# Layer 1's first pass in three parts around a run-time branch, with two chunks kept from attention and three tiles loaded early

## The chip, the cores and the metric

The kernel runs on one core of one Trainium2 chip. The metric is the device time of one execution in microseconds (us), as the median of the runs shown; less is better. The profile comes from one further execution of the same program, and every time inside it counts from the start of its span.

## What is computed

The input `x` is an image of 256 x 256 tokens with 128 channels, in fp32. Four layers follow each other; each adds its result to `x`, and each takes `_gn(x)`, a group normalization over the whole image, so that a layer's first product needs the statistics of all that the layer before has written. The change lies at the seam between layers 0 and 1.

```
x = x + L0(_gn(x))     # layer 0: gated attention along each row, 4 heads of 32
x = x + L1(_gn(x))     # layer 1, cut to what matters here:
    a = sigmoid((x @ Wa1 + ba1) * (x @ Wa2 + ba2))     # 16 channels
    b = sigmoid((x @ Wb1 + bb1) * (x @ Wb2 + bb2))     # 16 channels
    z = einsum('bikc,bkjc->bijc', a, b)
    out = sigmoid(x @ Wg + bg) * (_ln(z) @ Wz + bz)
...                    # layers 2 and 3 follow
```

## The kernel before, in words

All activations are held channel-first: 128 channels on the 128 partitions, tokens along the free axis. The 65536 tokens are cut into 32 chunks of 2048 (`SC`), 1 MB each in fp32; DRAM holds them in `x1T`. Attention works on 64 groups of 1024 tokens (`GT`), so chunk s is made of the groups 2s and 2s+1.

**Attention.** One loop over half groups, j from 0 to 132, is written out by hand in issue order (`manual_schedule`). Its tail has no new scores: from j = 128 on it only finishes what is in flight. `close` takes the statistics of a finished half group (`bn_stats`) and, at the second half, stores the group to `x1T`: on SP's DMA queue, and for the last two groups on ACT's. `gn_part` at j = 130 merges all statistics but those of the last group.

**Layer 1's first pass.** It takes the chunks in the order `order1` = 0, 16, 1, 17, ... For each chunk PE makes two products of 32 rows for each of four pieces (line 937), ACT adds a bias (946), DVE multiplies (947), ACT takes the sigmoid (923), and SP stores the 256 KB result `p3_ab` to `abD` (928). The chunks are held in a ring of 13 tiles of 1 MB. The stack of on-chip memory puts these tiles over attention's buffers: the first six lie on the six `p2_e` buffers, the next on `p2_es`, `pick`, `p2_rb` and `p2_u`, the last two reach into `p2_x`. The first eight loads are issued as soon as those buffers are done with. The ring is refilled by SP: the load of chunk i+13 waits for PE's products of chunk i (line 861). SP's instructions run in order, and a transfer is issued only when the one eight before it in the round of eight completion semaphores has landed.

**The flag's branch.** Attention leaves out the subtraction of the row maximum. The statistics show whether anything overflowed: `chk_ok`, `chk_n` and `chk_bad` make the flag (lines 871 to 876), every engine loads it (877), and `tc.If(again > 0)` (878) runs `general_attention`, a slow and safe version, where it is set. With these inputs it is never set. In that case every engine jumps over the body into a short block which keeps the semaphores in step: for each semaphore that the body would have raised, one instruction waits until everything issued before the branch has raised it, and then adds what the body would have added. For the eight completion semaphores of the transfers SP does this, one after the other. The body reloads the ring's tiles, so the first products on these tiles after the branch wait for the raised values. In the program as built, PE's wait for the third chunk, for instance, is for the value 1632, where everything before the branch makes 1600 and the short block adds 32.

**Around it.** After the branch come the group means and the scaled weights (`gn_groups`, lines 197 to 208, then 901 to 912), and then the pass. When the last `abD` store has landed, the z stage loads `abD` again (lines 971 and 975) and goes on.

Of the kernel before, what the change touches and what calls it, by code (L numbers as in the profile page):

```python
# [32 lines left out]
def kernel(ctx: ExitStack, tc: tile.TileContext, a: dict, out: bass.AP):  # L33
# [142 lines left out]
    def gn_part(stats, lo, hi, name):  # L176

        mv = const.tile([P, 2], F32, name=name)
        nc.vector.bn_aggr(mv, stats[:, lo:hi, :].rearrange("p n s -> p (n s)"))
        return mv  # L180
# [11 lines left out]

    def gn_groups(mv, name):

        with tc.tile_pool(name=name + "_ps", bufs=1, space=PSUM, reuse_waits="tile") as ps, tc.tile_pool(name=name + "_sb", bufs=1, reuse_waits="tile") as sb:
            pm = ps.tile([P, 1], F32, name=name + "_pm")
            nc.tensor.matmul(pm, lhsT=gmat, rhs=mv[:, 0:1], start=True, stop=True)
            mean = const.tile([P, 1], F32, name=name + "_mean")
            nc.vector.tensor_copy(mean, pm)
            d = sb.tile([P, 1], F32, name=name + "_d")  # L200
            nc.vector.tensor_sub(d, mv[:, 0:1], mean)
            nc.vector.scalar_tensor_tensor(d, d, d, mv[:, 1:2], ALU.mult, ALU.add)
            pv = ps.tile([P, 1], F32, name=name + "_pv")
            nc.tensor.matmul(pv, lhsT=gmat, rhs=d, start=True, stop=True)
            sd = sb.tile([P, 1], F32, name=name + "_sd")
            nc.scalar.activation(sd, pv, AF.Sqrt, bias=epst)
            rstd = const.tile([P, 1], F32, name=name + "_rstd")
            nc.vector.reciprocal(rstd, sd)
        return mean, rstd
# [3 lines left out]
    def new_stats(name):  # L213
        return stats_pool.tile([P, T // CK, 6], F32, name=name, tag="gn_stats")
# [37 lines left out]
    def spans(x):  # L252
        return [(h * GT, x[h]) for h in range(2)] if isinstance(x, tuple) else [(0, x)]

    raw = tri_pool.tile([P, NH + 2, 2, N], F32, name="tri_raw")
    triT, rsT = raw[:, 0:NH], raw[:, NH + 1]
    with tc.tile_pool(name="x0", bufs=1, reuse_waits="tile") as xres, tc.tile_pool(name="p0", bufs=3, reuse_waits="tile") as sb:
        tags = [("x", X_BUFS)] * 5 + [("xn", 2)] * 2 + [("rs", 1)]
# [346 lines left out]

    stats1 = new_stats("stats1")
    rzD = dram.tile([N // 4, 16, N], F32, name="rzD")
    NG = N // G  # L610
    with tc.tile_pool(name="p2e", bufs=6, reuse_waits="tile") as eb, tc.tile_pool(name="p2c", bufs=1, reuse_waits="tile") as cs:
        with att_scope, tc.tile_pool(name="p2u", bufs=2, reuse_waits="tile") as sb, tc.tile_pool(name="p2S", bufs=2, space=PSUM, reuse_waits="tile") as psS, tc.tile_pool(name="p2z", bufs=1, space=PSUM, reuse_waits="tile") as psZ, tc.tile_pool(name="p2M", bufs=3, space=PSUM, reuse_waits="tile") as psM, ExitStack() as by_hand:
            rows = {}

            def load(g):
                load_x(g)
# [135 lines left out]
            def close(g, c):  # L752
                x1 = groups[g]["x"]
                nc.vector.bn_stats(stats1[:, g * 2 + c, :], x1[:, c * CK : (c + 1) * CK])
                if c == 1:
                    queue = nc.sync if g < NG - 2 else nc.scalar
                    queue.dma_start(x1T[:, g * GT : (g + 1) * GT], x1)
                    del groups[g]

# [18 lines left out]
            for j in range(2 * NG + 5):  # L780
# [60 lines left out]
                    close(*out)  # L841
                if half == 0 and 0 <= g - 2 < NG:
                    divide(g - 2)
                if j == 2 * NG + 2:
                    mv_first = gn_part(stats1, 0, 2 * NG - 2, "gn1_a")
                if half == 1 and g + 2 < NG:
                    prepare(g + 2)

# [1 line left out]

    order1 = [b + h * NSC // 2 for b in range(NSC // 2) for h in range(2)]
    SLOTS, FIRST = 13, 8
    x1_scope = ExitStack()
    slots = [x1_scope.enter_context(tc.tile_pool(name=f"x1_{i}", bufs=1, reuse_waits="tile")) for i in range(SLOTS)]
    xs = {}

    def load1(s, slot):
        xs[s] = slots[slot].tile([P, SC], F32, name="x1", tag="x1")  # L860
        nc.sync.dma_start(xs[s], x1T[:, s * SC : (s + 1) * SC])

    for i in range(FIRST):
        load1(order1[i], i)


    mv1 = gn_merge(mv_first, gn_part(stats1, 2 * NG - 2, 2 * NG, "gn1_b"), 1.0 - 1.0 / NG, "gn1_mv")
    flag = const.tile([P, 1], mybir.dt.int32, name="flag")
    with tc.tile_pool(name="chk", bufs=1, reuse_waits="tile") as sb, tc.tile_pool(name="chkps", bufs=1, space=PSUM, reuse_waits="tile") as ps:
        ok = sb.tile([P, 2], F32, name="chk_ok")  # L870
        nc.vector.tensor_scalar(ok, mv1, 0.0, 0.0, ALU.mult, ALU.is_equal)
        pn = ps.tile([P, 2], F32, name="chk_n")
        nc.tensor.matmul(pn, lhsT=ones, rhs=ok, start=True, stop=True)
        bad = sb.tile([P, 2], F32, name="chk_bad")
        nc.vector.tensor_scalar(bad, pn, P - 0.5, None, ALU.is_lt)
        nc.vector.tensor_tensor(flag, bad[:, 0:1], bad[:, 1:2], ALU.max)
    again = nc.values_load(flag[0:1, 0:1], min_val=0, max_val=1)
    with tc.If(again > 0):
        general_attention(
            tc, dict(xT=xT, rsD=rsD, mbD=mbD, triD=triD, x1T=x1T),  # L880
            dict(wf=wf, wo=wo, b_g=b_g, b_o=b_o, cqkg=cqkg, cv=cv, mneg=mneg, ident=ident),
            dram, stats1,
        )
        nc.vector.bn_aggr(mv1, stats1.rearrange("p n s -> p (n s)"))
        for s in order1[:FIRST]:
            nc.sync.dma_start(xs[s], x1T[:, s * SC : (s + 1) * SC])

    m1, r1 = gn_groups(mv1, "gn1")
    v1 = const.tile([P, 32], F32, name="v1")
    v2 = const.tile([P, 32], F32, name="v2")
    vb1 = const.tile([P, 1], F32, name="vb1")
    vb2 = const.tile([P, 1], F32, name="vb2")
    wgf = const.tile([P, D], F32, name="wgf")
    bgf = const.tile([P, 1], F32, name="bgf")
    with tc.tile_pool(name="f1ps", bufs=1, space=PSUM, reuse_waits="tile") as ps:
        for w, wf_, ub, vb, n in ((u1, v1, ub1, vb1, "1"), (u2, v2, ub2, vb2, "2")):  # L900
            nc.vector.tensor_scalar(wf_, w, r1, None, ALU.mult)
            pb = ps.tile([P, 1], F32, name="f1_u" + n)
            for q in range(4):
                nc.tensor.matmul(pb[32 * q : 32 * q + 32, :], lhsT=wf_, rhs=m1, start=True, stop=True)
            nc.vector.tensor_tensor(vb, ub, pb, ALU.subtract)
        nc.vector.tensor_scalar(wgf, wg1, r1, None, ALU.mult)
        pb = ps.tile([P, 1], F32, name="f1_g")
        nc.tensor.matmul(pb, lhsT=wgf, rhs=m1, start=True, stop=True)
        nc.vector.tensor_tensor(bgf, bg1, pb, ALU.subtract)

    c1neg = const.tile([P, 1], F32, name="c1neg")
    nc.vector.tensor_scalar(c1neg, mv1[:, 0:1], -1.0, None, ALU.mult)
    usum = const.tile([P, 2 * NSC], F32, name="usum")
    qsum = const.tile([P, NSC], F32, name="qsum")

    with x1_scope:
        with tc.tile_pool(name="p3", bufs=3, reuse_waits="tile") as sb, tc.tile_pool(name="p3ps", bufs=3, space=PSUM, reuse_waits="tile") as ps, tc.manual_schedule():
            halves, done = [], []

            def close3():  # L920
                s, s1 = halves.pop(0)
                ab = sb.tile([P, CK], F32, name="p3_ab", bufs=12)
                nc.scalar.activation(ab, s1, AF.Sigmoid)
                done.append((s, ab))

            def store3():
                s, ab = done.pop(0)
                nc.sync.dma_start(abD[:, s * CK : (s + 1) * CK], ab)

            for i in range(FIRST, SLOTS):  # L930
                load1(order1[i], i)
            for i, s in enumerate(order1):
                p1 = ps.tile([P, CK], F32, name="p3_1")
                p2 = ps.tile([P, CK], F32, name="p3_2")
                for pp, w in ((p1, v1), (p2, v2)):
                    for c in range(4):
                        nc.tensor.matmul(
                            pp[32 * c : 32 * c + 32, :], lhsT=w, rhs=xs[s][:, c * CK : (c + 1) * CK],
                            start=True, stop=True,
                        )  # L940
                if i + SLOTS < NSC:
                    load1(order1[i + SLOTS], i % SLOTS)
                if len(done) > 1:
                    store3()
                s1 = sb.tile([P, CK], F32, name="p3_s1")
                nc.scalar.activation(s1, p1, AF.Identity, bias=vb1)
                nc.vector.scalar_tensor_tensor(s1, p2, vb2, s1, ALU.add, ALU.mult)
                halves.append((s, s1))
                if i:
                    close3()  # L950
            close3()
            while done:
                store3()

# [66 lines left out]
        with tc.tile_pool(name="p4", bufs=3, reuse_waits="tile") as sb, tc.tile_pool(name="p4psg", bufs=2, space=PSUM, reuse_waits="tile") as psg, tc.tile_pool(name="p4psz", bufs=2, space=PSUM, reuse_waits="tile") as psz, tc.manual_schedule():  # L1023
# [43 lines left out]
            for i, s in enumerate(order):  # L1067
# [34 lines left out]
                    nc.sync.dma_start(x2T[:, s_ * SC : (s_ + 1) * SC], xs[s_])  # L1102
                j = i - 4 + SLOTS
                if i > 3 and j < NSC:
                    load1(order[j], (j + 7) % SLOTS)
            sum4()
            nc.sync.dma_start(x2T[:, s * SC : (s + 1) * SC], xt)

# [917 lines left out]
```

## Time and profile before

| what | value |
|---|---|
| median of 3 runs | 3259.66 us (3257.19 to 3260.97) |
| profiled execution, its own time | 3258.13 us |
| its span | 3256.4 us |
| mean granted TensorE clock | 0.968 |
| scores of attention end, tail begins | about 1441 us |
| layer 1's loads of chunks begin | 1453.6 us |
| branch | 1479.3 to 1484.0 us |
| first pass on PE | 1490.4 to 1558 us |
| first load of the z stage | 1567.2 us |

In the profile, SPq, PEldq and the like are the sequencers of the engines. A row of the windows' table gives a stretch, its length, the busy time of each engine in it with the number of its instructions, the granted TensorE clock, the busy share of the 16 DMA engines and the GB/s that they moved. A row of the waits gives who waited for whom, the us in total, how often, and the longest. A row of the timeline gives start, length, engine, line, operation and tiles.

### The profile page before, as it was taken

How to read it: one execution, taken by the hardware profiler on the slowest of the kernel's cores; microseconds unless marked ns; L12 is line 12 of the kernel's file. 1: busy time of each engine (PE TensorE's matmuls, PEld its weight loads, DVE VectorE, ACT ScalarE, POOL GpSimd, SP SyncE). 2: the span in 40 equal slices, each digit the busy share in tenths (PEclk: the TensorE clock that was granted, in tenths of full speed). 3: DMA queues.
4: the chain of work that ended last, by engine and by line, in shares of the span. 5: the costliest groups of instructions: out<-in, count | busy, mean ns of one | idle time of the engine just before them, and what ended most of it. 6: DMA issues, size and time to landing. Idle time of an engine off the chain costs nothing. (4 is left out here: it accounts for less than half of the span.)

```text
span 3256.4 us, 51714 instructions
## 1 busy us (share of the span) xinstructions
PE 3052.1 (94%) x19908; PEld 1634.6 (50%) x19908; DVE 2264.2 (70%) x2617; ACT 2030.0 (62%) x2272; POOL 1725.2 (53%) x925
## 2 busy tenths in 40 slices
PE   5699999999999999996799799999999989979998
PEld 4535555555555555552533344444699933324444
DVE  5657888888888888883546455454455588858887
ACT  3577777777777777754467545444344457757776
POOL 5005777777777777760268000000255568848887
PEclk8899999999999999998899899999999999989999
DMA  9972333333333333339679677666699989986775
GB/s 353 412 299 95 107 124 112 105 125 112 105 124 113 105 123 114 105 134 392 220 305 413 238 275 306 250 253 259 262 351 353 346 316 388 389 290 195 235 231 153
DMA packets 291220, 748.13 MB, mean 230 GB/s; under 512 B 68441, under 2 KB 138731, under 8 KB 242171
## 3 DMA queue, kind: packets, MB, share of 16 engines
q1 hardware_dynamic: 282065, 731.02, 61.6%
q0 software_dynamic: 6064, 12.21, 1.0%
q8 instruction: 160, 2.62, 0.3%
q10 hardware_dynamic: 2840, 1.54, 0.2%
q14 instruction: 91, 0.75, 0.1%
HBM read 457.29 MB, written 287.38 MB: 229 GB/s over the span
## 5 line engine op out<-in xcount | busy, mean ns | idle before, releaser
L680 POOL TENSOR_TENSOR p_es<-p_e 128x1024 f32<-128x1024 f32 x256 | 603.3, 2367 | 304.7 <-ACT p_e L678 234.8
L670 DVE TENSOR_TENSOR p_e<-p_S,tri_raw 128x1024 f32<-128x1024 f32 x512 | 609.2, 1212 | 144.3 <-PE p_S L660 144.2
L678 ACT ACTIVATE p_e<-p_e,mbT 128x1024 f32<-128x1024 f32 x512 | 551.9, 1138 | 62.0 <-DVE p_e L670 62.0
L1231 PE MATMUL p_pm<-p_zn,wf 128*128 128x512 f32 x1040 | 448.7, 593 | 1.9 <-ACT p_a L1266 1.9
L645 PE MATMUL p_mm<-p_xn,w 128*128 128x512 f32 x764 | 404.7, 613 | 0.1
L1231 PEld LDWEIGHTS p_pm<-p_zn,wf 128*128 128x128 f32 x1040 | 196.8, 190 | 253.9 <-issue 246.6
L660 PE MATMUL p_S<-p_qk 32*128 32x256 f32 x4096 | 295.8, 401 | 3.3 <-DVE p_e L670 3.3
L1328 POOL MEMSET k<- 128x512 f32 x1 | 0.5, 525 | 522.4 <-PE p_pm L1231 522.4
L660 PEld LDWEIGHTS p_S<-p_qk 32*128 32x128 f32 x4096 | 186.2, 184 | 159.3 <-PE p_mm L636 91.7
L1984 PE MATMUL tp_z<-p_B,tp_at 128*128 128x256 f32 x1024 | 250.7, 388 | 0.8 <-DMA p_B<-bD 0.6
L693 PE MATMUL p_o<-p_e,p_vg 128*32 128x256 f32 x4096 | 249.2, 384 | 0.0
L627 POOL TENSOR_TENSOR p_xn<-p_xn,p_rs 128x1024 f32<-128x1024 f32 x62 | 148.8, 2400 | 182.5 <-ACT p_xn L622 97.9
L1359 POOL TENSOR_TENSOR k<-k,p_sq 128x512 f32<-128x512 f32 x128 | 163.3, 1276 | 136.0 <-ACT p_sq L1357 136.0
L1984 PEld LDWEIGHTS tp_z<-p_B,tp_at 128*128 128x128 f32 x1024 | 185.1, 190 | 21.8 <-DVE tp_at L1975 1.6
L645 PEld LDWEIGHTS p_mm<-p_xn,w 128*128 128x128 f32 x764 | 125.3, 191 | 104.1 <-issue 88.3
L1358 DVE TENSOR_TENSOR k<-tp_z,k 128x512 f32<-128x512 f32 x128 | 88.5, 692 | 127.0 <-ACT p_sq L1357 127.0
L693 PEld LDWEIGHTS p_o<-p_e,p_vg 128*32 128x32 f32 x4096 | 120.5, 110 | 110.0 <-ACT p_vg L651 41.5
L651 ACT ACTIVATE p_vg<-p_mm,bgh 128x512 f32<-128x512 f32 x128 | 88.0, 687 | 135.5 <-PE p_mm L645 135.5
L1355 ACT COPY p_K<-tp_z 128x512 f32<-128x512 f32 x128 | 75.0, 586 | 155.2 <-PE tp_z L1984 155.2
L1270 DVE SCALAR_TENSOR_TENSOR p_b<-p_pm,b2w,p_b 128x1024 f32<-128x1024 f32 x64 | 82.1, 1284 | 122.2 <-PE p_pm L1231 107.8
L636 PEld LDWEIGHTS p_mm<-w,p_xn 128*128 128x128 f32 x1016 | 134.2, 192 | 61.3 <-issue 60.6
L649 ACT ACTIVATE p_qk<-p_mm,cqkg 128x512 f32<-128x512 f32 x127 | 87.3, 687 | 122.5 <-PE p_mm L645 122.1
(394 smaller groups left out, 6068.6 us busy)
## 6 DMA issues: line engine op xcount, KB each, us to landing
p_x<-x2T SPq DMA_DIRECT2D x60, 1024.0 KB
x<-x1T SPq DMA_DIRECT2D x51, 1024.0 KB
p_x<-in_x_dram SPq DMA_DIRECT2D x32, 1024.0 KB
p_x<-xT SPq DMA_DIRECT2D x64, 512.0 KB
p_rs<-rsD SPq DMA_DIRECT2D x64, 512.0 KB
x2T<-x SPq DMA_DIRECT2D x32, 1024.0 KB
aD<-p_a SPq DMA_DIRECT2D x32, 1024.0 KB
bD<-p_b SPq DMA_DIRECT2D x32, 1024.0 KB
```

What stands on the lines that cost most here:

```text
L627: nc.gpsimd.tensor_tensor(xn, xn, groups[g]["rs"], ALU.mult)
L636: nc.tensor.matmul(pm[:, k * D : (k + 1) * D], lhsT=t["xn"][:, b * P : (b + 1) * P], rhs=wf[:, 2 * D : 3 * D], start=True, stop=True,)
L645: nc.tensor.matmul(pm, lhsT=w, rhs=t["xn"][:, cs_], start=True, stop=True)
L660: nc.tensor.matmul(Ss[h // 2][:, h % 2, u, :], lhsT=t["k"][hp, r * N + u * P : r * N + (u + 1) * P], rhs=t["q"][hp, r * N : (r + 1) * N], ...
L670: nc.vector.tensor_tensor(e[:, :, 2 * p : 2 * p + 2, :].rearrange("p u h n -> p h u n"), Ss[p], triT[:, 2 * p : 2 * p + 2, :, :], ALU.add,)
L678: nc.scalar.activation(e[:, u, :, :], e[:, u, :, :], AF.Exp, bias=mbT[:, u, i : i + 1])
L680: nc.gpsimd.tensor_tensor(es, e[:, 0, :, :], e[:, 1, :, :], ALU.add)
L693: nc.tensor.matmul(t["o"][hp, r % 2, :], lhsT=t["v"][:, r * 2 + u, hp], rhs=e[:, u, h, :], start=(u == 0), stop=(u == 1),)
L1231: nc.tensor.matmul(pm[:, c, :], lhsT=wf2[:, i, :], rhs=zns[s][:, k * CK : (k + 1) * CK], start=True, stop=True)
L1358: nc.vector.tensor_tensor(k1, pz, k1, ALU.add)
L1359: nc.gpsimd.tensor_tensor(k2, k2, sq, ALU.add)
L1984: nc.tensor.matmul(pz[:, t, :], lhsT=at[:, u, t * P : (t + 1) * P], rhs=Bc[:, u, :], start=(u == 0), stop=(u == 1))
```

## The change

- The order of layer 1's chunks becomes 14, 30, 15, 31, 0, 16, 1, 17, ... Chunks 30 and 31, the last that attention makes, are not loaded: the pass reads them from attention's own `p2_x` tiles (`kept`). They are still stored.
- Chunk 14 is loaded at j = 126 into the two `p2_xn` tiles, chunk 15 at j = 126 into a `p2_qk` tile, chunk 0 at j = 128 into the `tri_raw` tile (`fill1`). Attention's right-hand pools stay open until the first five chunks are done.
- The first statistics are merged at j = 129 without the last two groups (before: at j = 130 without the last one), and a one-column square root on ACT stands there.
- The ring's first 11 tiles are opened right after attention; their loads go out in the order of attention's buffers, the last-used `p2_e` buffer's tile first. The other two tiles (`LATE`) lie on `p2_x` and are opened, and loaded, after the first part.
- The group means, the weights and the flag are computed before the branch. `chk`, `d` and `sd` are taken from the constant pool.
- The pass runs in three parts: chunks 0 to 4 of the order with their results in attention's `p2_vg` tiles, chunks 5 to 17, then the branch, then chunks 18 to 31. The body of the branch now also computes the first 18 chunks again and reloads 13 tiles.

```diff
+    order1 = [14, 30, 15, 31] + [b + h * NSC // 2 for b in range(NSC // 2 - 2) for h in range(2)]
+    def fill1(i, x):
+        s = order1[i]
+        xs[s] = x
+        for at, xh in spans(x):
+            at += s * SC
+            nc.sync.dma_start(xh, x1T[:, at : at + xh.shape[-1]])
...
-                    del groups[g]
+                    kept[g] = groups.pop(g)["x"]
...
-                if j == 2 * NG + 2:
-                    mv_first = gn_part(stats1, 0, 2 * NG - 2, "gn1_a")
+                if j == 2 * NG - 2:
+                    fill1(0, tuple(gt_tile(f"x1_e{h}", "xn", 2) for h in range(2)))
+                    x1_e = att_sb.tile([P, 2, GT], F32, name="x1_e2", tag="qk", bufs=2)
+                    fill1(2, x1_e.rearrange("p a t -> p (a t)"))
+                if j == 2 * NG:
+                    fill1(4, tri_pool.tile([P, SC], F32, name="x1_e4", tag="tri_raw"))
+                if j == 2 * NG + 1:
+                    nc.scalar.activation(const.tile([P, 1], F32, name="root_a"), epst, AF.Sqrt)
+                    mv_first = gn_part(stats1, 0, 2 * NG - 4, "gn1_a")
...
-    SLOTS, FIRST = 13, 8
+    SLOTS, LATE, FIRST, SPLIT = 13, 2, 5, 18
...
+    ring = [3, 4, 5, 6, 7, 8, 9, 10, 0, 1, 2]
...
-    for i in range(FIRST):
-        load1(order1[i], i)
+    for i in (0, 1, 2, 8, 9, 10, 3, 4, 5, 6, 7):
+        load1(order1[FIRST + i], i)
+    for i, g in ((1, NG - 4), (3, NG - 2)):
+        xs[order1[i]] = kept[g], kept[g + 1]
...
+    weights1("gn1")
+    flag = const.tile([P, 1], mybir.dt.int32, name="flag")
+    chk = const.tile([P, 4], F32, name="chk")
...
+                for i in range(lo, hi):
+                    s, p1, p2, s1, ab = piece_ab(i, ps, make)
+                    if FIRST <= i < NSC - SLOTS:
+                        load1(order1[i + SLOTS], (i - FIRST) % SLOTS)
+                    if len(done) > 1:
+                        store3()
+                    nc.scalar.activation(s1, p1, AF.Identity, bias=vb1)
+                    nc.vector.scalar_tensor_tensor(s1, p2, vb2, s1, ALU.add, ALU.mult)
+                    halves.append((s, s1, ab))
+                    if i > lo:
+                        close3()
+                close3()
+                while done:
+                    store3()
...
+        pass_a(0, FIRST, lambda name: spare.pop(0))
+        att_scope.close()
+        place += [slot_pool(i) for i in range(SLOTS - LATE, SLOTS)]
+        slots += place[SLOTS - LATE :]
+        for i in range(SLOTS - LATE, SLOTS):
+            load1(order1[FIRST + i], i)
...
+        with tc.tile_pool(name="p3a", bufs=3, reuse_waits="tile") as sb:
+            pass_a(FIRST, SPLIT, make3(sb))
+
+        again = nc.values_load(flag[0:1, 0:1], min_val=0, max_val=1)
+        with tc.If(again > 0):
...
+            for s in order1[SPLIT : SPLIT + SLOTS]:
+                nc.sync.dma_start(xs[s], x1T[:, s * SC : (s + 1) * SC])
+
+        with tc.tile_pool(name="p3b", bufs=3, reuse_waits="tile") as sb:
+            pass_a(SPLIT, NSC, make3(sb))
```

## The prediction

> **What bounds the kernel now.** I read the page first, for the slices in which PE is not at 9, and then only the stretch from attention's tail (about 1441 us) to the z stage's first load (1567.2 us), since nothing else changes. The windows' table over that stretch says what is full.
>
> ```profile
> 1459.00:1478.80 19.80, 7.08 (x17) 3.70 (x15) 11.31 (x17) 0.00 (x0) 0.00 (x0) 0.68 1.00 413
> 1478.80:1482.20 3.40, 0.12 (x1) 0.03 (x1) 0.32 (x2) 1.28 (x1) 0.00 (x0) 0.50 0.15 27
> 1482.20:1490.40 8.20, 2.16 (x22) 1.94 (x23) 1.75 (x10) 0.26 (x1) 0.00 (x0) 0.50 0.98 380
> 1490.40:1494.00 3.60, 3.60 (x25) 0.95 (x28) 0.31 (x2) 0.69 (x1) 0.00 (x0) 0.61 1.02 430
> 1494.00:1508.00 14.00, 14.00 (x136) 3.92 (x132) 6.29 (x9) 10.83 (x17) 0.00 (x0) 1.00 0.97 372
> 1508.00:1545.00 37.00, 32.30 (x296) 8.85 (x292) 12.34 (x17) 19.49 (x33) 0.00 (x0) 1.00 1.02 422
> ```
>
> The DMA engines are the bound. Their share is 0.97 to 1.02 in all rows but one, the branch, where it falls to 0.15 for 3.4 us; DMA share, not PE, is the column to follow. PE idles until 1490.4, then runs flat for a while, and from 1508 on waits for data. The timeline of SP's queue gives the pace.
>
> ```profile
> 1453.60 45.65 SPq L861 DMA_DIRECT2D x<-x1T  x17
> ...
> 1534.39 0.33 SPq L861 DMA_DIRECT2D x<-x1T  x1
> ...
> 1537.44 0.33 SPq L861 DMA_DIRECT2D x<-x1T  x1
> ...
> 1540.58 0.33 SPq L861 DMA_DIRECT2D x<-x1T  x1
> ...
> 1543.65 0.33 SPq L861 DMA_DIRECT2D x<-x1T  x1
> ...
> 1567.21 1.74 SPq L971 DMA_DIRECT2D z_ab<-abD  x4
> ```
>
> One load and one store take 9.26 / 3 = 3.09 us. A load alone is 1.049 MB at 430 GB/s, 2.44 us, so a store counts 0.65 us. PE needs less: in the timeline 264 records, 16 a chunk, take 28.56 us, 1.73 us a chunk. The waits show what the flag costs, and what SP waits for.
>
> ```profile
> DVE chk_ok L871 <- DMA x1T<-p_x: 5.9, 1, 5.9
> ```
>
> ```profile
> SPq L861 <- DMA x<-x1T: 29.4, 15, 2.8
> ...
> SPq L877 <- DVE flag L876: 17.2, 1, 17.2
> ```
>
> Last, the branch's own line.
>
> ```profile
> L878 PEldq COMPARE_BRANCH  x1: 3699/3699/3699, 1480.0 to 1480.0; - x1
> L878 DVEq COMPARE_BRANCH  x1: 72/72/72, 1480.0 to 1480.0; - x1
> L878 SPq COMPARE_BRANCH  x1: 50/50/50, 1480.2 to 1480.2; - x1
> L878 ACTq EVENT_SEMAPHORE  x1: 17/17/17, 1480.4 to 1480.4; - x1
> L878 DVEq EVENT_SEMAPHORE  x1: 21/21/21, 1483.2 to 1483.2; - x1
> ```
>
> ```profile
> L878 SPq EVENT_SEMAPHORE  x8: 17/17/17, 1480.4 to 1480.9; - x8
> ```
>
> These eight are SP's waits for all transfers issued before the branch. They cost 17 ns each only because the DMA engines had run dry at 1478.8. That is the line on which the forecast rests.
>
> **The change part by part.**
>
> *Traffic taken out.* Of 32 loads after 1453.6, 28 remain: chunks 30 and 31 are kept, 14 and 15 move to about 1440, where the DMA share is 0.14 (1440 to 1450). 4 x 2.44 = 9.8 us of DMA time go. What the moved ones cost: three transfers on SP before the 4 KB `rzD` stores at 1448.3; 2.1 MB and the 0.5 MB store before them need 6.1 us from 1440, so they have landed before SP issues anything that matters. Zero; if that cover went, `p2_rb` would be late, and POOL's division at 1455.9 with it. Chunk 0's load (j = 128) takes the place of the first load at 1453.6.
>
> *The first loads.* They wait for the same buffers. The tile now first lies under the last row's `p2_e`; before, that tile was the fourth, issued at 1455.92. Meanwhile the 2.44 us of chunk 0's load fill the engines. Zero.
>
> *Statistics.* `gn_part` (3.56 us on DVE, 1464.83) moves to about 1461, ahead of the last group's division, which PE's last products need. Before, it lay in DVE's wait for them, so about 0.6 us come on: the statistics are ready at 1472.8 instead of 1472.2. The square root's table load (1.28 us) falls into ACT's idle time after 1453.4.
>
> *Flag and weights.* The 5.9 us wait of `chk_ok` goes with its buffer. The chain from the first group product (1484.00) to the first chunk (1490.40) took 6.4 us, 2.6 of them an issue gap of PE (at line 908) after the branch; without that gap 3.8, and the flag's own product adds 1.2 by its rows (1478.04 to 1479.31): the first chunk starts at 1472.9 + 5.0, about 1478, instead of 1490.4. This is 12 us on PE but not on the path, as the DMA engines were busy until 1478.8 and will now be busy longer.
>
> *The engines' run up to the branch.* 1478.8 was the end of eight loads and three 0.5 MB stores. Now chunk 0 and three more loads come on: 1478.8 + 4 x 2.44 = 1488.6. The five stores of the first part follow (3.3): 1491.9. Their last one is ready 12.4 us after PE's start (before: 1490.40 to SP's fifth store, 1502.78), at 1490.4, and SP's two late loads stand behind it and start then, so no gap. Two loads (4.9) and 13 pairs (40.2) give 1537.0. When the queue was shallow before, between 1494 and 1508, it moved 372 instead of 422 GB/s, a loss of 14 x 50 / 422 = 1.7 us; the same thin moment comes at 1492, so I take it: T0 = 1538.7. Without it, 1537.0; with it twice, 1540.4.
>
> *The branch in mid pass.* PE ends chunk 17 at about 1478 + 3.4 + 17 x 1.73 = 1511. All engines jump while transfers run, and the jump (PE's 3.70 us) is covered by what follows: SP's eight waits hold until every earlier load and store has landed, T0, and PE's products on chunks 18 to 30 wait for values that only SP's eight additions (0.6 us) raise. Behind SP's wait stand the load of chunk 31 and 14 stores; behind PE's, everything. PE idles some 28 us, the DMA engines run dry once more, and the 14 chunks that used to ride along under the transfers now come after them.
>
> The Trainium skill, page "Runtime: NRT & Kernel Launch", section "Instruction fetch mechanics", says that a taken branch out of the prefetched pages costs a fetch by DMA. The row shows it for PE (3.70 us), with DVE's gap from 1480.0 to 1483.2; by the rule, with the DMA engines full, the fetch could be longer here, and by row or rule the sum stays, since 28 us cover it.
>
> *The last part.* PE starts at 1538.7 + 0.6 = 1539.3, cold: before, after an idle stretch (clock 0.50), the first chunk took 3.4 us (1490.40 to the refill's issue at 1493.77), so 3.4 + 13 x 1.73 = 25.9, to 1565.2. The last result follows 2.1 us later (1500.64 to 1502.78 for the fifth chunk). Its store, 256 KB on an empty queue: at least 0.65 plus the 1.37 us between the first `rzD` store's issue and the read that needs it (1448.27, 1449.64), 2.0; at most the last store of before, 4.4 (1562.78 to 1567.21), which had others ahead. I take 3.0, nearer the empty queue. The z stage loads at 1570.3 against 1567.2: **+3.1 us**, with 2.0 and 4.4 and T0's ends between 0.4 and 6.2.
>
> *Behind that* nothing changes: z, and the ring's slots after it, hold the same 13 chunks, and the constant-pool tiles remove no wait elsewhere (in the other normalizations `d` and `sd` waited only for their data).
>
> The sum: 3258.13 + 3.1 = 3261.2 for the profiled execution, which stands 1.5 under the median; against the median, 3262.8.
>
> **The rivals.**
>
> *Faster: the branch does not drain.* If PE took tiles as they land, the transfers would go through: 1537.0 + 1.7 + one load 2.44 + 14 stores 9.1 = 1550.2, and the tail to 1551.5: 15.7 us less, 3244. For it: PE has 4 tiles or more in hand at 1511, and the jump itself is cheap. Against it: SP's eight waits, and PE's wait values. Anything between is possible only if T0 comes early, and T0 is a sum of bytes.
>
> *Slower: the late loads start late.* SP issues the two late loads and all refills behind the fifth store, so each us by which the first chunk starts later than about 1479 leaves the DMA engines empty and moves T0. With 3.1 already there, it passes 0.2% (6.5 us) once the first chunk starts after 1482.5. For it: PE's 2.6 us issue gap in this very chain, and five serial hops between DVE, PE and ACT. Against it: that gap came after a jump. With the full old chain of 6.4, the flag's 1.2 and one more fetch of 3.7 the start is 1484.2, 5 us late: 3268.
>
> *Slower: PE stays at half clock after its long idle.* 14 chunks at twice 1.73 would add 13 x 1.73 = 22 us, 3285. Against it: the clock was 1.00 from 1494 on, 3.6 us after the start.
>
> **How the numbers follow.** About 0.2%, 6.5 us, is what a measurement of this kernel can tell from no change. My forecast, the drain, holds 0.75, with its own range of 3258 to 3269 (the terms' ends, 3260 and 3266, and 2 to 3 us for what is in no row); about 0.13 lies above 6.5 us. The fast rival has 0.10, the late start 0.12, the slow clock 0.03. So faster 0.11, slower 0.15 + 0.13, about 0.28, same 0.61. The range for 8 in 10 takes the forecast's own and part of both sides: 3252 to 3272.
>
> **What would show it.** Right: SP's eight semaphore instructions on the branch's line spread over about 10 us and end near 1539; PE idle before it for over 20 us, then 14 chunks at 1.73 us without waiting for a load; a second hole in the DMA share, from about 1539 to 1565; the first chunk at about 1478 and no hole at 1480. Wrong: PE's products running on across the branch; a hole at 1492; the z stage's first load before 1561 or after 1574. What would make it wrong is a T0 other than 1537 to 1541, or a PE that does not wait for SP.

## The result and the profile after

The changed kernel takes 3271.69 us (median of 9 runs, 3267.94 to 3276.30) against 3261.29 us (9 runs, 3257.19 to 3263.94): ratio 1.0032, 95% interval 1.0024 to 1.0040, so 10.4 us (7.8 to 13.0) slower. The profiled execution has a span of 3270.0 us at a mean clock of 0.966.

For every kernel below I use one length from SP's timeline, the **seam**: from the store of attention's group 61 (the last `x1T<-p_x` row of SP's queue) to the z stage's first load. It leaves out what differs before it. The changed kernel was late long before this seam: by 3.6 us at the last product of the first, transfer-bound stage (149.58 against 146.02), ahead of the first changed instruction, and by 2.95 us from about 400 us on. Executions differ by that much in the first stage: in the runs below, whose code up to there is all but the same, the store of group 61 stands between 1453.4 and 1457.3. It stands at 1453.15 before and at 1456.10 after, the first load of z at 1567.21 and 1580.60: the seam is 114.1 us before and 124.5 us after, **+10.4 us**, as much as the medians differ.

The windows' table of the changed kernel; the columns after the length are PE, PE's weight loads, DVE, ACT, POOL, the granted clock, the DMA share and GB/s:

```profile
1460.00:1492.50 32.50, 23.28 (x120) 9.36 (x120) 16.77 (x34) 4.23 (x6) 1.16 (x1) 0.68 1.01 410
1492.50:1505.00 12.50, 9.02 (x69) 2.44 (x73) 3.66 (x5) 7.29 (x13) 0.00 (x0) 0.86 0.37 123
1505.00:1517.50 12.50, 12.50 (x124) 3.82 (x120) 5.87 (x8) 9.03 (x16) 0.00 (x0) 1.00 1.01 423
1517.50:1550.00 32.50, 2.70 (x28) 0.59 (x20) 1.64 (x3) 3.04 (x5) 0.00 (x0) 0.59 1.02 410
1550.00:1555.00 5.00, 3.95 (x24) 1.17 (x28) 0.37 (x1) 0.69 (x1) 0.00 (x0) 0.58 0.15 53
1555.00:1580.00 25.00, 21.83 (x204) 6.53 (x196) 10.57 (x15) 16.30 (x27) 0.00 (x0) 1.00 0.53 190
```

The hole that the kernel before had at its branch is gone, and there are two others. That at 1550, followed by 25 us at a share of 0.53, was forecast: the drain. That from 1492.5 to 1505 was not: 12.5 us x (1 - 0.37) = 7.9 us of the DMA engines' time. SP's timeline of the same kernel shows what stands in it:

```profile
1458.88 23.52 SPq L882 DMA_DIRECT2D x<-x1T  x11
1488.52 13.19 SPq L951 DMA_DIRECT2D abD<-p_spare  x5
1501.80 3.81 SPq L882 DMA_DIRECT2D x<-x1T  x6
...
1554.57 0.35 SPq L882 DMA_DIRECT2D x<-x1T  x1
1556.66 22.05 SPq L951 DMA_DIRECT2D abD<-p_ab  x14
1580.60 1.74 SPq L1025 DMA_DIRECT2D z_ab<-abD  x4
```

Five stores of 256 KB take SP 13.2 us, and the loads behind them go out only at 1501.80. The row of the waits, from 1480 to 1510, and three rows of ACT's timeline say what the stores wait for:

```profile
ACT p_spare L946 <- DMA abD<-p_spare: 8.2, 3, 5.4
```

```profile
1494.58 0.63 ACT L946 ACTIVATE p_spare<-p_spare 128x512 f32<-128x512 f32 x1 [5.37 <-DMA abD<-p_spare]
1497.34 0.63 ACT L946 ACTIVATE p_spare<-p_spare 128x512 f32<-128x512 f32 x1 [1.41 <-DMA abD<-p_spare]
1500.07 1.29 ACT L946 ACTIVATE p_spare<-p_spare 128x512 f32<-128x512 f32 x2 [1.38 <-DMA abD<-p_spare]
```

The sigmoids of chunks 1, 2 and 3 each wait until the store of the result before theirs has landed; those of chunks 0 and 4 do not. The reason lies in one line of the change: `att_sb.tile(..., tag="vg", bufs=3)[:, c, :] for _ in range(3) for c in range(4)` calls `tile` twelve times. That gives not three tiles cut into four pieces but twelve tiles that take turns on three buffers, and the pieces `c` of different tiles hide it. In the program as built the results of chunks 0 to 3 all lie in the buffer at address 192480, that of chunk 4 in another one.

At the branch PE waits for SP, as the prediction said. Two rows of its line, and the row of the waits from 1510 to 1582:

```profile
L985 SPq EVENT_SEMAPHORE  x8: 17/17/17, 1550.9 to 1553.0; - x8
L985 PEldq COMPARE_BRANCH  x1: 6297/6297/6297, 1518.1 to 1518.1; - x1
```

```profile
PE p L935 <- SPq L985: 30.9, 1, 30.9
```

### The profile page after: what moved, and what is told of

Its sections match the earlier page's. It is cut to its first block, busy times and chain, and to the rows that moved or that the text cites. A ratio compares the mean times of both kernels' runs of the same rounds, so it can differ in the third digit from the quotient of the medians.

```text
span 3270.0 us, 51691 instructions
## 1 busy us (share of the span) xinstructions
PE 3057.3 (93%) x19908; PEld 1636.2 (50%) x19908; DVE 2263.5 (69%) x2617; ACT 2030.3 (62%) x2273; POOL 1724.8 (53%) x925
## 5 line engine op out<-in xcount | busy, mean ns | idle before, releaser
L1412 DVE TENSOR_TENSOR k<-tp_z,k 128x512 f32<-128x512 f32 x128 | 88.6, 692 | 127.3 <-ACT p_sq L1411 127.3
```

What stands on the lines that cost most here:

```text
L1412: nc.vector.tensor_tensor(k1, pz, k1, ALU.add)
```

## The experiments

All ratios are to the kernel before, timed beside each run on the same chip.

| run | seam, us | against before | time ratio (95% interval) |
|---|---|---|---|
| changed kernel | 124.5 | +10.4 | 1.0032 (1.0024 to 1.0040) |
| three tiles | 116.7 | +2.7 | 1.0009 (1.0000 to 1.0018) |
| SPLIT 8 | 115.9 | +1.8 | 1.0001 (0.9993 to 1.0010) |
| three tiles, SPLIT 8 | 108.4 | -5.7 | 0.9978 (0.9968 to 0.9988) |
| three tiles, no branch | 111.2 | -2.9 | 0.9988 (0.9980 to 0.9997) |
| three tiles, no branch, one pool | 100.6 | -13.4 | 0.9957 (0.9942 to 0.9972) |
| three tiles, SPLIT 8, loads behind the branch | 103.0 | -11.0 | 0.9962 (0.9949 to 0.9975) |
| three tiles, branch in its old place | 114.4 | +0.4 | 0.9995 (0.9986 to 1.0004) |
| before, flag's tiles in the constant pool | 112.8 | -1.3 | 1.0008 (0.9999 to 1.0016) |
| three tiles, one pool, branch behind chunk 17 | 119.1 | +5.1 | 1.0011 (1.0002 to 1.0020) |
| before, no branch | 107.0 | -7.1 | 0.9974 (0.9964 to 0.9983) |

0.001 of the ratio is 3.3 us. The seam of one execution and the ratio agree within 4 us everywhere, mostly within 2. A ratio rests on 9 to 12 executions of its run, but on 6 in the run with one pool and no branch, and on 5 in the one with the loads behind the branch. The kernel before stood at 3261.3 us beside the changed kernel, and at 3259.9, 3262.8 and 3259.4 beside the others, so a time in us that was expected from another group of runs can be off by up to 3 us for that alone. Ratios and seams decide below.

### Three tiles

```diff
-        spare = [
-            att_sb.tile([P, 4, CK], F32, name="p3_spare", tag="vg", bufs=3)[:, c, :] for _ in range(3) for c in range(4)
-        ]
+        three = [att_sb.tile([P, 4, CK], F32, name="p3_spare", tag="vg", bufs=3) for _ in range(3)]
+        spare = [t[:, c, :] for t in three for c in range(4)]
```

> Change: the buffers of the first part are three tiles cut into four pieces each, instead of twelve tiles that share three buffers. Theory A (in the changed kernel each sigmoid of the first part waits for the store of the result before it, because they share a buffer, so the five stores go out one at a time and the late loads behind them start late): the window 1492.5 to 1505 of the changed kernel has a DMA share of 0.37, 12.5 x 0.63 = 7.9 us empty; this hole goes, the waits of the sigmoids on the stores go, T0 comes 7 to 8 us earlier, and the time is 3271.7 - 7.9 = 3263.8 (3262 to 3266), some 2.5 us over before. Rival B (the late loads are late because they stand behind the stores on SP, whose first store stands behind eleven loads; the buffers only show it): the hole stays, 3271.7 within 2. Rival C (the drain costs more than forecast, and the hole is made up within it): the hole goes but T0 stays, 3271.7 within 2.

Measured: 3261.51 us, just below the 3262 to 3266 of theory A, but 2.9 us over before by the ratio (0 to 5.9) where 2.5 were expected; the seam is 7.8 us shorter than the changed kernel's. SP's timeline and the window of the hole in this run:

```profile
1483.90 5.72 SPq L951 DMA_DIRECT2D abD<-p_spare  x5
1489.72 5.64 SPq L882 DMA_DIRECT2D x<-x1T  x6
...
1570.51 1.74 SPq L1024 DMA_DIRECT2D z_ab<-abD  x4
```

```profile
1490.00:1502.50 12.50, 12.50 (x124) 3.52 (x120) 5.36 (x8) 8.88 (x16) 0.00 (x0) 1.00 1.03 414
```

The five stores take 5.7 us instead of 13.2, the loads follow at once, the DMA share is 1.03, and what is won is the hole. Theory A holds, B and C fall: SP's order is the same in both kernels, and the hole is not. Two lines of buffers cost 7.5 us of the 10.4, by the ratios.

### SPLIT 8, with the twelve and with the three tiles

`SPLIT` is the number of chunks ahead of the branch.

```diff
-    SLOTS, LATE, FIRST, SPLIT = 13, 2, 5, 18
+    SLOTS, LATE, FIRST, SPLIT = 13, 2, 5, 8
```

> Change: SPLIT is 8 instead of 18, with the twelve-tile buffers of the changed kernel. Forecast's view (SP's waits drain the queue, and what costs is that the chunks in hand and their stores come after the drain with little left to load beside them): with the branch after chunk 7, eleven loads and 24 stores come after the drain, 11 x 2.44 + 24 x 0.65 = 42.4 us of transfers, as much as PE needs for 24 chunks (3.4 + 23 x 1.73 = 43.2), so only about 4 us of the drain are lost; by the prediction's sum T0 is 1491.9 + 4.9 + 3 x 3.1 = 1506 and the z stage loads at 1506.6 + 43.2 + 2.1 + 3.0 = 1555 instead of 1570.3, some 14 us less (-12 to -16): 3271.7 - 14 = 3258. Rival (the drain costs the same wherever it stands, one refill of the queue): 3271.7 within 3.

> Change: both, three tiles cut in pieces and SPLIT 8. If the hole of 7.9 us and the place of the drain add up (theory A and the forecast's view): 3271.7 - 7.9 - 14 = 3250, faster than before by 11. If the drain at chunk 7 already waits for what the hole delays, so that only one counts: about 3258. If the drain's place does not matter: as the three tiles alone, 3264.

Measured: 1.0001 with the twelve tiles, 10 us less than the changed kernel instead of 14; 0.9978 with three tiles, 17.6 us less instead of 22, and 7.2 us faster than before. The place of the drain decides, and the two effects add up: with the twelve tiles the seam goes from 124.5 to 115.9, with three from 116.7 to 108.4. What fell short shows in two windows of the run with three tiles:

```profile
1500.00:1507.50 7.50, 0.00 (x0) 0.00 (x0) 0.00 (x0) 0.00 (x0) 0.00 (x0) 0.50 0.99 357
1507.50:1515.00 7.50, 5.20 (x36) 1.58 (x40) 0.75 (x1) 1.38 (x3) 0.00 (x0) 0.63 0.35 112
```

The end of the drain moves little for its time (357 GB/s), and then the DMA engines have little to do for 7.5 us, 4.9 us of it empty, until PE's first chunk gives SP a refill to issue, at 1513.38. PE goes on at 1509.80, 56.4 us after the store of group 61, where my sum gave 53.5.

### No branch

```diff
-        again = nc.values_load(flag[0:1, 0:1], min_val=0, max_val=1)
-        with tc.If(again > 0):
...
```

> Change: three tiles cut in pieces, and the flag's load and the branch with the general attention are left out (the flag is still computed; the kernel then has no path for inputs that need it). It prices the drain: by the prediction's rival without a drain the z stage's first load comes 15.7 us before that of the kernel before, so 3261.3 - 15.7 = 3245.6, some 18 us less than with three tiles and the drain at chunk 17. If the drain were nearly free (the transfers bound all of it): 3260 to 3264, as with three tiles alone.

Measured: 0.9988, 3255.81 us. Neither: 5.7 us less than with the branch, where 18 were expected, and no faster than the run that keeps its branch behind chunk 7. So my price for the drain, or my picture of what holds the last 14 chunks, was wrong. ACT's timeline of this run:

```profile
1542.35 0.63 ACT L946 ACTIVATE p_ab<-p_s 128x512 f32<-128x512 f32 x1 [26.90 <-DMA abD<-p_ab]
```

With no branch in the program, the first sigmoid of the last part still stands for 26.9 us, for a store. The last part opens its own pool, `p3b`, over the place of `p3a`. In the program as built its first result, chunk 18's, lies at the address of the last result of the part before, chunk 17's, and the sigmoid waits for the store of that one, which stands in SP's order behind all loads but the last. So there seem to be two holds at the same place, one hidden behind the other; the next run tests it.

### No branch, one pool

```diff
-        with tc.tile_pool(name="p3a", bufs=3, reuse_waits="tile") as sb:
-            pass_a(FIRST, SPLIT, make3(sb))
...
-        with tc.tile_pool(name="p3b", bufs=3, reuse_waits="tile") as sb:
-            pass_a(SPLIT, NSC, make3(sb))
+        p3_scope = ExitStack()
+        p3 = p3_scope.enter_context(tc.tile_pool(name="p3", bufs=3, reuse_waits="tile"))
+        pass_a(FIRST, SPLIT, make3(p3))
+        pass_a(SPLIT, NSC, make3(p3))
+        p3_scope.close()
```

> Change against the run without a branch: chunks 5 to 17 and chunks 18 to 31 draw their buffers from one pool that stays open, instead of a second pool over the first one's place. In the run without a branch ACT's first sigmoid behind chunk 17 waited 26.9 us for a store of the part before, until 1542.35, so PE stood as long as with the branch. Theory (two things hold the last 14 chunks, the branch's drain and the second pool's buffers, and either alone is enough): that wait goes, PE runs on behind chunk 17 until its twelve result buffers are full and then goes on with each store; the transfers set the end: 28 loads x 2.44 + 32 stores x 0.65 = 89.1 us from 2.5 us after the store of group 61, 2 to 3 us of losses, the z stage's first load some 97 us after that store instead of 111.2: 14 us less, 3255.8 - 14 = 3242. Rival (PE is held by the twelve result buffers and SP's order in any case): the same wait at another place, 3253 to 3256.

Measured: ratio 0.9957, 14 us less than before; the seam falls by 10.5 us against the run above, to 100.6 where 97 was expected. The median, 3253.46 us, lies among the rival's 3253 to 3256, but before stood at 3262.8 beside it, not at 3259.9; by the ratios the run is 10 us faster than the one above. The wait of 26.9 us is gone, and the longest wait of a sigmoid for a store is 2.1 us, by the row of the waits from 1475 to 1572:

```profile
ACT p_ab L946 <- DMA abD<-p_ab: 16.2, 9, 2.1
```

The second pool was the second hold. The missing 3 to 4 us lie at the end, where the transfers no longer fill the engines: 18 us at 330 GB/s in place of 418 are 3.8 us.

```profile
1500.00:1540.00 40.00, 34.23 (x316) 9.31 (x308) 13.51 (x18) 20.50 (x34) 0.00 (x0) 1.00 1.02 418
1540.00:1558.00 18.00, 6.70 (x48) 1.47 (x40) 4.23 (x6) 6.96 (x12) 0.00 (x0) 0.85 0.86 330
```

### One pool, with the branch

The same pool with the branch behind chunk 17; general attention is left out of its body.

> Change against one pool without a branch: the branch is there again, behind chunk 17, with a body that recomputes the 18 chunks but holds no general attention (which does not fit beside the open pool; the kernel has no path for inputs that need it). It tells what the branch alone holds, without the second pool's buffers. If either alone is enough to hold the last 14 chunks: the seam, from the store of group 61 to the z stage's first load, is as long as with three tiles, 116.7 us in place of 100.6, and the ratio to before 1.000 to 1.002. If the second pool was needed for it: PE runs on behind chunk 17 before the drain has ended, the seam 101 to 108, ratio 0.996 to 0.998.

Measured: ratio 1.0011, seam 119.1. The branch alone holds as long as branch and pool together (31.0 us of PE's time, waits from 1475 to 1572):

```profile
PE p L935 <- SPq L985: 31.0, 1, 31.0
```

Against the run without it, the drain behind chunk 17 costs 18.5 us of the seam, 17.6 by the ratios. The seam is 2.4 us longer than with two pools, and the traces show where 2.0 of them lie: SP's eight waits end 88.5 us after the store of group 61 in both runs, but PE goes on 86.6 us after it with two pools and 88.6 us after it here. In the program as built PE's first wait behind the branch is for the first of SP's eight semaphores there, for the seventh here. The ratios do not tell the two runs apart.

### Loads behind the branch

```diff
-    SLOTS, LATE, FIRST, SPLIT = 13, 2, 5, 18
+    SLOTS, LATE, FIRST, SPLIT = 13, 2, 5, 8
...
-                    if FIRST <= i < NSC - SLOTS:
+                    if SPLIT <= i < NSC - SLOTS:
...
-        for i in range(SLOTS - LATE, SLOTS):
-            load1(order1[FIRST + i], i)
...
-            for s in order1[SPLIT : SPLIT + SLOTS]:
+            for s in order1[SPLIT : FIRST + SLOTS - LATE]:
                 nc.sync.dma_start(xs[s], x1T[:, s * SC : (s + 1) * SC])
...
+        for i in range(SLOTS - LATE, SLOTS - FIRST + SPLIT):
+            load1(order1[FIRST + i], i % SLOTS)
```

> Change against three tiles with SPLIT 8: the two late loads and the three refills of chunks 5 to 7 are issued behind the branch, not before it. If what the drain costs is the time in which the DMA engines run dry (there from about 1508 to 1515, the drain's end, the engines' way through the branch and PE's first chunk before its first refill), five loads that wait for nothing on PE fill its end, and the drain ends earlier by up to 5 x 2.44 = 12 us: 11 loads and 8 stores before it, until some 46 us after the store of group 61, then 1.9 us of the branch, then 16 loads and 24 stores, 54.7 us, and 1.5 to the z stage's first load: 104 us after that store against 108.4 there, 4 us less, 3249. Rival (nothing is won, since the same bytes still wait on one drain): 3253 within 2.

Measured: 3251.97 us, ratio 0.9962: **12.4 us faster than before (8.2 to 16.6), and by the two ratios 23 us faster than the changed kernel**, with the branch and general attention in it. The seam is 103.0 us; 104 was expected, and it was 108.4 with the loads ahead of the branch. By time alone the rival is not out: the intervals of the two ratios overlap (0.9978 and 0.9962), and 3251.97 is one of the rival's times too (3253 within 2). The seam, one execution of each, and the windows at its branch speak for the gain:

```profile
1495.00:1500.00 5.00, 2.42 (x12) 0.68 (x16) 0.00 (x0) 0.38 (x1) 0.00 (x0) 0.73 0.46 123
1500.00:1510.00 10.00, 10.00 (x96) 3.20 (x92) 3.99 (x6) 6.22 (x11) 0.00 (x0) 0.96 1.02 428
```

The drain is over at 1497.4 (the last of SP's eight), five loads that wait for nothing go out at once, and the engines lose 5 x (1 - 0.46) = 2.7 us. It is within 2.4 us, by the seam, of the run with one pool and no branch.

### The branch in its old place

```diff
+        again = nc.values_load(flag[0:1, 0:1], min_val=0, max_val=1)
+        with tc.If(again > 0):
+            nc.vector.bn_aggr(mv1, stats1.rearrange("p n s -> p (n s)"))
+            weights1("gn1g")
+            for i in range(FIRST + SLOTS - LATE):
...
         three = [att_sb.tile([P, 4, CK], F32, name="p3_spare", tag="vg", bufs=3) for _ in range(3)]
```

> Change against three tiles: the flag's branch stands where the kernel before has it, ahead of the first chunk, and all 32 chunks come after it (27 of them from one pool). The body of the branch holds no general attention here, only the reloads; the kernel has no path for inputs that need it. It tells what the kept and early chunks bring alone. The drain now waits for the eleven first loads, 1488.6 by the prediction's sum, PE starts behind it, and the late loads come behind the fifth store, 12.4 us after PE's start, at about 1503: a hole of some 10 us; then 16 loads and 27 stores, 56.6 us, and 3 to the z stage's first load: 1563 against 1567.2 before, 4 us less than before, ratio 0.9987, 3256. If the place of the branch does not matter against the traffic saved: 9.8 us less than before, 3250. If the hole is as long as the whole first part: no less than before, 3260.

Measured: ratio 0.9995, no difference from before, seam 114.4: the third case. The windows:

```profile
1490.00:1500.00 10.00, 7.05 (x48) 3.06 (x52) 1.50 (x2) 2.64 (x3) 0.00 (x0) 0.63 0.04 18
1500.00:1510.00 10.00, 10.00 (x100) 4.46 (x96) 4.50 (x6) 7.66 (x14) 0.00 (x0) 1.00 0.55 179
```

14 us of the engines' time are empty. The saved loads are worth nothing here: they are paid back in a hole in which the DMA engines wait for PE's first chunks (at a clock of 0.63) and for the stores ahead of the next loads.

### Two edits of the kernel before

First only the flag's tiles:

```diff
-    with tc.tile_pool(name="chk", bufs=1, reuse_waits="tile") as sb, tc.tile_pool(name="chkps", bufs=1, space=PSUM, reuse_waits="tile") as ps:
-        ok = sb.tile([P, 2], F32, name="chk_ok")
+    chk = const.tile([P, 4], F32, name="chk")
+    with tc.tile_pool(name="chkps", bufs=1, space=PSUM, reuse_waits="tile") as ps:
+        ok, bad = chk[:, 0:2], chk[:, 2:4]
```

> Change: the kernel before, with only the flag's small tiles in the pool of constants, so that the 5.9 us for which chk_ok waited for a store go. By the prediction's view the flag is then ready some 6 us earlier, but SP's waits at the branch hold until the transfers in front of it have landed, which before was at 1478.8 as well: no change, ratio 0.999 to 1.001. Rival (the flag's wait set the branch, and with it the start of PE): 3 to 6 us less, ratio 0.998 to 0.999.

Measured: 1.0008 (0.9999 to 1.0016), no gain. The wait of 5.9 us was covered by the transfers: the first result is stored 41.0 us after the store of group 61 instead of 46.2, and still the seam falls by no more than 1.3 us.

Then without the branch:

> Change: the kernel before without the flag's load and the branch (no path for inputs that need the general attention). It splits what the one-pool run without a branch won over before, 13.4 us of the seam, into the traffic saved (four loads, 4 x 2.44 = 9.8 by the prediction) and before's own branch. If the parts add up: the hole of 3.4 us at a share of 0.15 (2.9 us) and up to 1.7 us of the thin stretch behind it go, 3 to 5 us less than before, seam 109 to 111, ratio 0.9985 to 0.9991. If before's branch was hidden: seam 114, ratio 1.000, and the traffic saved is worth 13. If before's branch cost all of it: seam 101, ratio 0.996, and the traffic saved is worth nothing.

Measured: ratio 0.9974, seam 107.0. The branch cost the kernel before 7.1 us of seam (8.5 by the ratio), twice what I read from its hole of 3.4 us. PE started at 1483.15 here instead of 1490.40. What is left of the change with no branch on either side, the four saved loads above all, brings 107.0 - 100.6 = 6.4 us of seam, not 9.8: the bytes are fewer by 4.2 MB, but the end of the pass fills the engines less (330 GB/s in the last 18 us of the run with one pool, 383 in the last 22 of this run):

```profile
1538.00:1560.40 22.40, 8.62 (x76) 2.00 (x66) 5.74 (x8) 8.99 (x16) 0.00 (x0) 0.87 0.96 383
```

## Why the prediction was right or wrong

The forecast was 3262.8 us, the range 3252 to 3272; 3271.7 lies in it, at its edge, and that owes much to luck: the drain's own range ended at 3269, and a hole that no term of the sum had happened to fit into the margin kept for the rivals. The sum had +3.1 us, measured are +10.4. "Same" had 0.61, and it became slower, which had 0.28. By its own signs the sum was wrong: there was a hole near 1492, T0 lay outside 1537 to 1541, and the z stage's first load came after 1574. The drain was there and cost about what the sum gave it; one step ahead of it failed. Point by point, all in the times of the profile before (2.95 us off the changed kernel, 0.62 off the run with three tiles):

| step | predicted | changed kernel | three tiles |
|---|---|---|---|
| first chunk on PE | 1478.0 | 1477.5 | 1476.4 |
| SP's five stores over, loads go on | 1490.4 | 1498.8 | 1489.0 |
| PE goes on behind the branch | 1539.3 | 1548.1 | 1539.7 |
| PE's last product ends | 1565.2 | 1573.9 | 1566.1 |
| z's first load | 1570.3 | 1577.7 | 1569.9 |

- **The step that failed** is in the engines' run up to the branch: "Their last one is ready 12.4 us after PE's start [...], at 1490.4, and SP's two late loads stand behind it and start then, so no gap." I read the buffers of the first part as twelve pieces of three tiles and gave its results no wait. They share buffers; the five stores were out at 1498.8, 8.4 us late, and the gap was 7.9 us. Run with three tiles, this table's last column follows the prediction within 1.6 us at every step, and its +2.7 us of seam stands against the predicted +3.1. The 12.4 us of this step carry a wrong label but hold: SP's store at 1502.78 is its third, and what ended at 1502.77 is ACT's fifth sigmoid, which is what the step needs; with three tiles the fifth result was ready 11.8 us after PE's start.
- **The rival** "late loads start late" named the place and the price (each us of delay of those loads is a us of T0) but not the cause. Its condition, a first chunk after 1482.5, was not met. I tied the fifth store to PE's start alone and left out what else can hold it, the buffers of the results.
- **The drain**: right in kind and price. PE stood 30.9 us ("some 28") until SP's waits let it go, then made 14 chunks in 25.8 us (25.9), with a second hole and a stretch of little traffic. SP's eight waits did not spread over about 10 us, though, but over 2.1. Taking the branch away with one pool gives back 16 to 18 us: the rival without a drain said 15.7 below before, and that run is 13.4 to 14.0 below it.
- **A hold I did not see**: the pool of the last part would have held PE without any branch. It did not change the sum, because the drain covers it, but the rival "the branch does not drain" could not have come true in this kernel: it needed 3244, and with three tiles and no branch the kernel takes 3255.8.
- **Terms that cancelled**: SP's last wait ended at 1550.1, 11.4 us after the predicted T0; 7.9 are the hole, and with three tiles it is still 3.0 late, as in the last 2 us of the drain the share falls to 0.1 (0.09 from 1551 to 1553 in the changed kernel). PE went on 2 us before the last of the eight, since in the program as built its first wait is for the first of them, and from the last store's issue to z's first load were 2.2 us instead of 3.0.
- **What costs nothing**: the first chunk came 0.5 us early, so the early loads and the first loads held nothing up. The statistics were complete at 1474.0, not at 1472.8, but the first product of the group means needs the mean alone and started at 1473.1. The flag's wait was worth nothing in the kernel before, as its own run showed.
- **The traffic saved** (9.8 us): 6.4 by the seams of the two kernels without a branch, which hold the rest of the change too.

## What to carry to other kernels

A buffer is a call, not a slice: where a comprehension calls for a tile per piece, look up in the program as built which results share an address, and which store each writer then waits for. A wait for everything in flight costs what can't be done beside transfers any more, so put it where the queue is short and where much is left to load, and keep some transfers that wait for no engine to issue right behind it (seams with three tiles: 116.7 us behind chunk 17, 108.4 behind chunk 7, 103.0 there with five loads behind it, but 114.4 ahead of the first chunk, where PE's first chunks held the next loads). A hold that is removed may stand in front of a second one at the same place: the run without the branch won 6 us, and only with the second pool gone as well did the price, 16 to 18 us, show.

## What the runs showed of the hardware

PE's jump over the branch took 3.70 to 6.30 us in the kernels whose body is long. In the run with the branch in its old place and a body without general attention and without the recomputed chunks, it took 0.37 us:

```profile
L969 PEldq COMPARE_BRANCH  x1: 369/369/369, 1479.0 to 1479.0; - x1
```

So a jump over a short body cost next to nothing. The Trainium skill, page "Runtime: NRT & Kernel Launch", section "Instruction fetch mechanics", says that a taken branch stalls where its target lies outside the pages in hand; these rows agree with it, though none of them shows which pages were in hand. Whether a long jump costs more beside running transfers, as the prediction thought it could, these runs leave open: it took 3.70 us at a DMA share of 0.46 (before), but 3.71 at a share of 1.02 (SPLIT 8 with the twelve tiles), 4.41 at 0.87 (loads behind the branch) and 5.97 to 6.30 at shares from 0.79 to 1.02 in the others. Where the branch stands in mid pass, the jump ended before SP's waits did. In the kernel before it ended later, at 1483.7 against 1480.9; what it cost there, no run shows apart from the rest of the branch.
